# New rates for TensorE in the clock that weaves two stages of a four-layer network

## The chip, the cores and the metric

The kernel runs on one core of one Trainium2 chip. The metric is the device time of one execution in microseconds; several executions are timed and their median is taken. The core's engines are TensorE (PE, matrix products into PSUM), VectorE (DVE), ScalarE (ACT), GpSimd (POOL) and the sync engine (SP), from which most DMA transfers are issued. [...]

## The reference

The input `x` has shape (16, 32, 128, 128), float32. Four layers each add a function of the group-normalised `x` to `x`:

```python
x = x + _L0_conv_ref(_gn(x), ...)   # row LSTM over skewed columns, 128 steps
x = x + _L1_conv_ref(_gn(x), ...)   # adder convolution 3x3 on quantised values
x = x + _L2_conv_ref(_gn(x), ...)   # 2-D Hartley transform, 32x32 modes mixed, back
x = x + _L3_conv_ref(_gn(x), ...)   # edge operators, conv1..conv7, pools, deconvs
```

The adder convolution computes, for each image, output channel f and pixel,

```python
out[n, f, i, j] = -sum over c, kh, kw of |q[n, c, i + kh, j + kw] - qw[f, c, kh, kw]|
```

with `q` and `qw` rounded to whole numbers between -127 and 127. The last layer normalises five edge operators of `x`, applies a 3x3 convolution to their 160 channels, three levels of max pooling with 3x3 convolutions, three 2x2 deconvolutions with 3x3 convolutions behind them, and multiplies the result by its input.

## The kernel before, in words

**Stages.** `stage0` computes the LSTM layer; it is over before the part that matters here. `rest` computes the other three layers. The adder convolution is done by `Differences`, the Hartley layer and the last layer by `After`.

**The maps.** An image is handled in two halves of 64 rows. For each half there are 72 maps (8 blocks of output channels by 9 taps), 16 x 2 x 72 = 2304 in all. A map is `max(q - w, 0)` of a tile of 128 partitions by 8192 or 8320 float16 values, made either by DVE (line 760, tile `d_dve`, three buffers) or by ACT (line 757, tile `d_act`, two buffers). For each map PE adds it up over channels with sixteen matmuls into four PSUM banks (`sums`, line 647). Nine times per half `linear` adds the part that is linear in `q` (line 662, sixteen matmuls). `keep_busy` puts matmuls with zero weights (line 677) where PE would stand idle: four to a bank, at most four banks a map. After the 72nd map `finish` adds the residual, collects statistics and stores the rows of `x2`.

**The two last layers.** `After.work` is a Python generator. Images are taken in four groups of four. For a group it goes through `forward` (transform: lines 1119, 1134, 1091), `mixing` (line 1206), `back` (lines 1270 and 1315), `statistics` (line 1420: products of rows, from which the variances of the edge operators come), the table of folded weights `wf` (lines 1551, 1553), `conv1` (a 5x5 convolution of 25 taps, line 1739, in 8 chunks of 16 rows, with edge parts at lines 1713 and 1756), the smaller convolutions (`conv`, line 1589), and the composed deconvolutions with their convolutions (`Composed.round`, lines 905 and 930), the last of which, in `last`, gives the output (lines 1868 and 1838). A group can begin only when its four images have come out of the adder convolution: `yield ("after", 4 * g + 3)`.

**What sets the order.** The order of the instructions on every engine is fixed when the program is written out. `Differences.run` keeps a clock for each engine: `weave.dve` and `weave.act` grow by `DVE_US` = 2.36 and `ACT_US` = 7.15 for each map, and a map goes to the engine that would end it first. `weave.pe` grows by `PE_US` for the sums of each map. After each map `weave.advance(due)` lets the generator of `After` go on as long as a further step fits on PE before the next sums are due:

```python
start = max(self.pe, self.ready)
if start + 1.0 > due + SLACK:
    return
us = self.step()
```

A step is what lies between two `yield`s. A positive number yielded is the time in us that the step's matmuls take on PE; it is added to `weave.pe`. A negative number is a wait of that many us before the generator goes on. `SUMMED` is a wait for PE's results. Work of DVE, ACT and SP that belongs to a step (evictions, loads, stores) is written out with the step or put off by `weave.later(us, step)`. `keep_order` then ties each engine to the order written. All numbers are the planner's[...].

Groups 0 to 2 are given to this weave; group 3 cannot be in it, since its images are the last. `drain(weave, end.weave)` writes out what is left of the weave and group 3, step by step, whichever of the two is behind on its own clock. When one of them is through, the other is `alone`: it then uses the PSUM banks of both and splits its evictions between DVE and ACT.

Of the kernel before, what the change touches and what calls it, by code (L numbers as in the profile page):

```python
# [483 lines left out]

DVE_US, ACT_US, PE_US = 2.36, 7.15, 1.0
LATE = 1.5
SLACK, CLOCK = 3.0, 1.0
SUMMED = ("summed",)  # L490
# [29 lines left out]
class Differences:  # L520
# [134 lines left out]
    def linear(self, acc, q, tap):  # L655

        kh, kw = tap // 3, tap % 3
        for j in range(4):
            for k in range(4):
                rows = slice(32 * k, 32 * k + 32)  # L660
                row = 16 * j + 4 * k + kh
                self.nc.tensor.matmul(
                    acc[k][32 * j : 32 * j + 32, :],
                    self.sel16[rows, 8, :],
                    q[rows, row : row + 4, kw : kw + W],
                    start=False,
                    stop=False,
                )
        self.weave.pe = max(self.weave.pe, self.weave.now) + 0.45

    def keep_busy(self, acc, q, until):


        start = max(self.weave.pe, self.weave.now)
        for k in range(min(int((until - start - 0.1) / 0.25), 4)):
            for j in range(4):
                self.nc.tensor.matmul(  # L677
                    acc[k][32 * j : 32 * j + 32, :], self.zero, q[:, :4, :W], start=False, stop=False
                )
            self.weave.pe = start + 0.25 * (k + 1)  # L680

    def run(self, tc, ctx, weave):
        nc, R, P = self.nc, self.R, self.P
# [149 lines left out]
class Composed:  # L833
# [60 lines left out]
    def round(self, src, n, acc, pick):  # L894

        nc, t = self.nc, self.t
        for tap in range(4):
            for j in range(4):  # L900
                par, row, rows, o = pick(j)
                top, left = row + par // 2 + tap // 2, par % 2 + tap % 2
                for blk in range(4):
                    part = slice(32 * blk, 32 * blk + 32)
                    nc.tensor.matmul(  # L905
                        acc[blk][32 * j : 32 * j + 32, o : o + rows * n],
                        t[part, 4 * par + tap, :],
                        src[part, top : top + rows, left : left + n],
                        start=tap == 0,
                        stop=tap == 3,  # L910
                        skip_group_check=True,
                    )
            yield rows * n / 512 * 0.2 + 0.95
            if tap != 2:
                continue
            for j in range(4):
                par, row, rows, o = pick(j)
                pr, pc = par // 2, par % 2
                col = o + pc * (n - 1)
                parts = [(2 + pc, slice(col, (rows - 1) * n + col + 1, n), rows)]  # L920
                if row == 0 and pr == 0:
                    parts += [(0, slice(o, o + n), n), (4 + pc, slice(col, col + 1), 1)]
                if row + rows == n and pr == 1:
                    at = (rows - 1) * n
                    parts += [(1, slice(o + at, o + at + n), n), (6 + pc, slice(at + col, at + col + 1), 1)]
                for k, to, width in parts:
                    for blk in range(4):
                        part = slice(32 * blk, 32 * blk + 32)
                        b = self.bd[part]
                        nc.tensor.matmul(  # L930
                            acc[blk][32 * j : 32 * j + 32, to],
                            t[part, 16 + k, :],
                            bass.AP(b.tensor, b.offset, [list(b.ap[0]), [0, width]]),
                            start=False,
                            stop=False,
                            skip_group_check=True,
                        )
            yield 0.4
# [20 lines left out]
class After:  # L959
# [71 lines left out]
    def forward(self, g):  # L1031
# [4 lines left out]
        with self.pool("t_m") as mp:  # L1036
# [9 lines left out]
            with self.pool("t_t") as tp, ExitStack() as rows:  # L1046
# [39 lines left out]
                def second(n):  # L1086

                    p = self.acc()
                    for q in range(4):
                        lhs = t1s[n][:, 4 * q : 4 * q + 4, :].rearrange("p c k -> p (c k)")  # L1090
                        nc.tensor.matmul(p[:, 32 * q : 32 * q + 32], lhs, cst["cas"], start=True, stop=True)

                    def out():
                        xm = tp.tile([128, 4, M1], F32, name="xm", bufs=self.buffers["xm"])
                        nc.vector.tensor_copy(xm.rearrange("p q k -> p (q k)"), p[:, :128])
                        weave.dve += 0.3
                        first = xm_d.offset + (4 * g + n // 2) * 32768 + 16384 * (n % 2)
                        to = bass.AP(xm_d.tensor, first, [[32, 128], [4096, 4], [1, 32]])

                        def store():  # L1100
                            nc.sync.dma_start(to, xm)
                            steps[n] = None
                            if n % 2:
                                steps[n] = weave.later(4.0, lambda: self.modes(g, n // 2, tp, xs, steps))

                        steps[n] = weave.later(2.0, store)

                    steps[n] = outs[n] = weave.summed(out)
                    return 1.45

                yield -4.0
                t1s, ta, ready = {}, {}, {}
# [2 lines left out]
                def first(n):  # L1115
# [8 lines left out]
                        weave.dve += 0.7  # L1124

                    ready[n, 0] = weave.summed(out)
                    return 1.05

                def turned(n):

                    weave.done(ready[n, 0])
                    p = self.acc()
                    for a in range(4):
                        nc.tensor.transpose(p[:, 128 * a : 128 * a + 128], ta[n][:, a, :], cst["ident128"])
                    ready[n, 1] = weave.summed(lambda: scaled(n, p))
                    return 1.5

                for n in range(10):
                    if n < 8:
# [56 lines left out]
    def mixing(self, g, xs, wp, wt):  # L1196
# [5 lines left out]
        for ky in range(M1):  # L1202
# [9 lines left out]
                )  # L1212
            if ky % 4 == 3 and len(wt) < M1 // 4:
                wt.append(self.weights(wp, len(wt)))
            yield 1.0
            if ky % 4 == 3 and 8 < ky < M1 - 1 and not weave.draining:
                yield -2.5
        yield SUMMED
        zs = wp.tile([128, 2, 4, 4, 32], F32, name="zs", bufs=1)
        for half in range(2):  # L1220
# [12 lines left out]
    def back(self, g, load):  # L1233
# [6 lines left out]
        with self.pool("t_z") as zp_, self.pool("t_r", ahead) as rp:  # L1240
# [23 lines left out]
            for oh in range(2):  # L1264
                pa = [self.acc() for _ in range(4)]
                for o in range(16):
                    for r in range(4):
                        for blk in range(4):
# [5 lines left out]
                                start=True,  # L1274
                                stop=True,
                            )
                    yield 1.1
                yield SUMMED
                for blk in range(4):
                    dst = o1[:, :, blk, 16 * oh : 16 * oh + 16].rearrange("p h o -> p o h")  # L1280
# [28 lines left out]
            for n in range(16):  # L1309
                s, half = n // 2, n % 2  # L1310
                pf = [self.acc() for _ in range(2)]
                for i in range(4):
                    for r in range(2):
# [5 lines left out]
                            start=True,  # L1319
                            stop=True,  # L1320
                        )
                yield 0.8
                if previous:
                    yield -3.2
                    take_out(*previous)
# [67 lines left out]
    def statistics(self, g, pool, frames, sides, out, tables):  # L1393
# [35 lines left out]
        for ch in range(H // 16):  # L1429
# [3 lines left out]
            for l in range(2, 18):  # L1433
# [7 lines left out]
                first, last = len(own), min(H - r, 3)  # L1441
                if first < last:
                    products(xp, l, slice(l + first, l + last), 64, 68 * first, False, r == H - 3)
                yield 0.5
                if l not in (9, 17):
                    continue

# [117 lines left out]
    def small_layers(self, cp, rp, y1, y2):  # L1565
# [11 lines left out]
        def conv(src, n, name, evict):  # L1577
            rows = min(n // 4, 512 // n)
            for r in range(0, n, 4 * rows):
# [3 lines left out]
                for tap in range(9):  # L1583
                    kh, kw = tap // 3, tap % 3
                    for j in range(4):
                        for blk in range(4):
# [6 lines left out]
                                start=tap == 0,  # L1593
                                stop=tap == 8,
                            )
                    yield rows * n / 512 * 1.0 + 0.15
                yield SUMMED
                for blk in range(4):
                    evict(r, rows, acc[blk][:, : rows * n], blk)
# [83 lines left out]
    def conv1(self, g, pool, frames, y1, sides, wf, b1):  # L1683
# [19 lines left out]
        for s, n in enumerate("lr"):  # L1703
            for tap in range(11):
                for j in range(4):
                    for blk in range(4):
# [11 lines left out]
                            stop=tap == 10,  # L1718
                            skip_group_check=True,
                        )  # L1720
                yield 0.6
        yield SUMMED
        cut = pool.tile([128, 4, 2, 8, 4], F32, name="cut")
        for blk in range(4):
# [4 lines left out]
        for ch in range(H // R):  # L1729
# [4 lines left out]
            for tap in range(25):  # L1734
# [11 lines left out]
                if edge and tap == 23:  # L1746
                    n, j, first, row = edge
                    for part, col, wide in ((n, 0, 5), (n + "l", 1, 2), (n + "r", W + 1, 2)):
                        width = W if wide == 5 else 1
                        o = first + (W - 1 if part == n + "r" else 0)  # L1750
                        for cut_tap in range(2 * wide + 1):
                            for blk in range(4):
# [8 lines left out]
                                    stop=False,  # L1761
                                    skip_group_check=True,
                                )
                            yield 0.3
                yield 1.15
            yield SUMMED
            if ch + ahead < H // R:
                for half in range(2):
# [275 lines left out]
```

## Time and profile before

| What | Value |
|---|---|
| Median of 3 runs | 6719.5 us (6713.72 to 6728.77) |
| Profiled execution | 6728.15 us |
| Its span, first to last instruction | 6726.4 us |
| Mean granted clock of TensorE | 0.919 |
| PE, DVE, ACT busy | 5379.0, 5537.9, 5464.8 us (80%, 82%, 81%) |
| Maps on DVE, on ACT | 1675 of 2360 ns, 629 of 7154 ns |
| `keep_busy` matmuls | 6720 |

The span can be cut by the sums of the maps (line 647), which run from 685 us to 5603 us: before them lies `stage0`, after them the drain. The groups' first transform matmuls (line 1119) start at 1838, 3434, 5029 and 5666 us. In the profile's counts an instruction on float32 operands appears as two matmuls, so that a tap of conv1, sixteen matmuls in the code, is x32. Busy times of PE are of pipelined matmuls with modelled ends: the distance from start to start tells what one costs. "PEld" is PE's loading of weights; "issue" is time in which an engine waited for nothing that the profile shows.

### The profile page before, as it was taken

The page shows a single profiled execution, that of the slowest core. Times are in us where ns is not written, and L with a number is a line of the kernel's source. Part 1 is how long each engine was busy: PE and PEld are TensorE (multiplying, and loading weights), DVE is VectorE, ACT ScalarE, POOL GpSimd, SP SyncE. Part 2 cuts the span into 40 slices and gives each one's busy share as a digit, 9 for nine tenths or more (in the row PEclk, how much of TensorE's full clock was granted, in tenths as well). Part 3 has the DMA queues.
Part 4 walks back from the last instruction along what each step waited for, and adds up shares of the span by engine and source line. Part 5 has one row for each costly group of instructions (what it writes and reads, how often), then busy time and mean ns, then how long its engine had stood idle before and what let it go on. Part 6 is the DMA issues. An engine that isn't in the chain of part 4 may idle for free.

```text
span 6726.4 us, 271378 instructions
## 1 busy us (share of the span) xinstructions
PE 5379.0 (80%) x127212; PEld 2798.3 (42%) x127212; DVE 5537.9 (82%) x6839; ACT 5464.8 (81%) x3210; POOL 63.0 (1%) x67
## 2 busy tenths in 40 slices
PE   3798777788777879997877878998787785886896
PEld 3675333333343433333333433333334442453574
DVE  7898999999999889998999989999899995144122
ACT  3998999999999989999999999999899993121112
POOL 0000000000000000000000000000000000000000
PEclk9999899999989989998999889999899897997897
DMA  7553312212253632213453552221354353355314
GB/s 318 204 190 123 81 49 64 61 31 66 71 140 113 178 94 60 62 38 72 101 147 93 174 149 68 66 63 42 87 128 138 103 155 119 125 188 141 83 39 107
DMA packets 380776, 728.20 MB, mean 108 GB/s; under 512 B 73284, under 2 KB 225348, under 8 KB 368772
## 3 DMA queue, kind: packets, MB, share of 16 engines
q1 hardware_dynamic: 372180, 676.41, 35.2%
q0 software_dynamic: 7040, 33.80, 1.5%
q8 instruction: 995, 16.30, 1.0%
q14 instruction: 129, 1.06, 0.1%
q10 hardware_dynamic: 432, 0.64, 0.0%
HBM read 510.69 MB, written 200.00 MB: 106 GB/s over the span
## 4 chain that ended last, share of the span: by engine, by line
issue 33%; PE 29%; DVE 20%; ACT 14%; DMA 3%; SPq 1%; POOL 0%; DVEq 0%; ACTq 0%; POOLq 0%
DVE d_dve L760 12%; PE acc L1739 11%; ACT d_act L757 9%; PE acc L647 8%; PE acc L905 3%; PE pg L223 3%; ACT gt L237 2%; DMA v<-fold_d 1%; PE acc L1589 1%; PE acc L1420 1%; ACT junk L198 1%; DVE y L1677 1%; DVE stat L124 1%; DMA x_in<-in_x_dram 1%; ACT th L247 1%
## 5 line engine op out<-in xcount | busy, mean ns | idle before, releaser
L757 ACT ACTIVATE d_act<-q,neg 128x8192 f16<-128x8192 f16 (+1 forms) x629 | 4450.5, 7154 | 102.7 <-PE acc L647 81.1
L760 DVE TENSOR_SCALAR d_dve<-q,qw 128x8192 f16<-128x8192 f16 (+1 forms) x1675 | 3864.3, 2360 | 214.5 <-PE acc L647 195.6
L647 PE MATMUL acc<-d_dve,sel 128*32 128x512 f16 x26800 | 1879.4, 404 | 436.3 <-DVE d_dve L760 344.6
L647 PEld LDWEIGHTS <-sel 128*32 128x32 f16 x36864 | 1021.0, 101 | 2124.4 <-issue 1475.8
L1739 PE MATMUL acc<-xp,wf 32*32 32x512 f32 x25600 | 1001.7, 611 | 32.6 <-issue 27.2
L647 PE MATMUL acc<-d_act,sel 128*32 128x512 f16 x10064 | 740.0, 416 | 345.2 <-ACT d_act L757 333.4
L1680 ACT ACTIVATE y<-pooled,b 32x128 f32<-32x128 f32 x472 | 188.7, 400 | 552.6 <-DVE pooled L1666 546.3
L1739 PEld LDWEIGHTS acc<-xp,wf 32*32 32x32 f32 x25600 | 417.6, 104 | 377.6 <-issue 295.8
L677 PE MATMUL acc<-q,zero 128*32 128x512 f16 x6720 | 484.2, 400 | 0.0
L905 PE MATMUL acc<-y,u_conv 32*32 32x256 f32 (+1 forms) x9728 | 358.7, 461 | 85.1 <-issue 68.7
L223 PE MATMUL pg<-h,wb 64*64 64x20 f32 (+15 forms) x8192 | 342.0, 306 | 58.0 <-DVE h L251 32.9
L237 ACT ACTIVATE gt<-pg,bias 128x20 f32<-128x20 f32 (+15 forms) x1024 | 332.7, 385 | 39.3 <-PE pg L223 37.1
L223 PEld LDWEIGHTS pg<-h,wb 64*64 64x64 f32 x8192 | 252.1, 151 | 133.5 <-DVE h L251 80.9
L677 PEld LDWEIGHTS <-zero 128*32 128x32 f16 x6720 | 200.6, 101 | 187.3 <-issue 42.7
L1868 DVE SCALAR_TENSOR_TENSOR xr<-acc,l_one,xr 128x512 f32<-128x512 f32 x128 | 87.2, 744 | 229.8 <-PE acc L905 179.7
L1420 PE MATMUL acc<-xp 32*64 32x204 f32 (+3 forms) x8576 | 240.8, 339 | 40.6 <-issue 40.5
L905 PEld LDWEIGHTS acc<-y,u_conv 32*32 32x32 f32 x9728 | 162.0, 109 | 216.9 <-issue 168.1
L1420 PEld LDWEIGHTS acc<-xp 32*64 32x64 f32 (+1 forms) x8576 | 169.1, 132 | 124.4 <-issue 118.9
L1838 ACT ACTIVATE xr<-xr,l_ms 128x1024 f32<-128x1024 f32 x64 | 68.7, 1146 | 182.1 <-DVE xr L1868 171.9
L223 PE MATMUL pg<-xn,wb 64*64 64x2 f32 (+63 forms) x4096 | 183.5, 290 | 25.6 <-issue 17.0
L1774 DVE TENSOR_TENSOR acc<-acc,cut 128x4 f32<-128x4 f32 x256 | 35.2, 164 | 200.6 <-PE acc L1739 198.3
L1589 PE MATMUL acc<-y,w_conv 32*32 32x512 f32 (+2 forms) x4608 | 153.6, 487 | 37.1 <-issue 28.9
(218 smaller groups left out, 3624.5 us busy)
## 6 DMA issues: line engine op xcount, KB each, us to landing
q<-q_d SPq DMA_DIRECT2D x128, 536.2 KB, 10.3
xp<-xn_d SPq DMA_DIRECT2D x64, 660.0 KB, 5.1
xp<-x_d SPq DMA_DIRECT2D x56, 640.0 KB, 5.3
xr<-xn_d SPq DMA_DIRECT2D x64, 528.0 KB, 11.3
x_in<-in_x_dram SPq DMA_DIRECT2D x16, 2048.0 KB, 14.7
xn<-in_xs_dram SPq DMA_DIRECT2D x64, 512.0 KB, 7.1
res<-in_x_dram SPq DMA_DIRECT2D x64, 512.0 KB, 8.6
x_d<-res SPq DMA_DIRECT2D x64, 512.0 KB, 4.8
```

The source lines that it names most:

```text
L223: nc.tensor.matmul(bank[c][q][64 * pair : 64 * pair + 64, :, :width], wb[half, 4 * kind + KIND[q]].rearrange("p b o -> p (b o)"), v[half], ...
L237: nc.scalar.activation(gt[:, q, :, :n], bank[c][q][:, :, :n], AF.Tanh if q == G else AF.Sigmoid, bias=bias[:, KIND[q] : KIND[q] + 1],)
L647: self.nc.tensor.matmul(acc[k][32 * j : 32 * j + 32, :], self.sel16[:, i // 9, :], d[:, row : row + 4, c : c + W], start=first, stop=last,)
L677: self.nc.tensor.matmul(acc[k][32 * j : 32 * j + 32, :], self.zero, q[:, :4, :W], start=False, stop=False)
L757: nc.scalar.activation(dst, src, AF.Relu, bias=self.neg[:, i : i + 1])
L760: nc.vector.tensor_scalar(dst, src, self.qw[:, i : i + 1], 0.0, ALU.subtract, ALU.max)
L905: nc.tensor.matmul(acc[blk][32 * j : 32 * j + 32, o : o + rows * n], t[part, 4 * par + tap, :], src[part, top : top + rows, left : left + ...
L1420: nc.tensor.matmul(gram[blk][j : j + width, at : at + n], xp[part, l, 2 + j : 2 + j + width], xp[part, rows, j : j + width + 4], start=sta ...
L1589: nc.tensor.matmul(acc[blk][32 * j : 32 * j + 32, : rows * n], wc[name][part, tap, :], src[part, at : at + rows, kw : kw + n], start=tap == 0,
L1680: nc.scalar.activation(d, s, AF.Identity, bias=bj)
L1739: nc.tensor.matmul(acc[blk][32 * j : 32 * j + 32, :], tap_of("all", tap)[rows], xp[rows, 4 * j + kh : 4 * j + kh + 4, kw : kw + W], start= ...
L1868: nc.vector.scalar_tensor_tensor(v, acc[blk].rearrange("p (b r w) -> p r w b", b=2, w=64), one[:, blk : blk + 1], v, ALU.add, ALU.mult,)
```

## The change

Only the numbers by which the planner's clock counts PE change; no operation is added to the computation or taken from it. `PE_US`, the price of the sums of a map, goes from 1.0 to 0.88; `linear` from 0.45 to 0.36; a bank of `keep_busy` from 0.25 to 0.22, as a price and as the measure of how many fit. The positive numbers that the steps of `After` yield are replaced: 1.45 to 1.2, 1.05 to 0.9 and 1.5 to 1.0 in `forward`; 1.0 to 0.3 in `mixing`, where the wait after every fourth step goes from 2.5 to 5.5; 1.1 to 0.35 and 0.8 to 0.4 in `back`; 0.5 to 0.38 in `statistics`; in `conv1` 1.15 to 1.06 for a tap, 0.6 to 0.35 and 0.3 to 0.1 for edge parts; and the two formulas of the smaller convolutions and deconvolutions both become `rows * n / 512 * 0.78 + 0.28`.

```diff
-DVE_US, ACT_US, PE_US = 2.36, 7.15, 1.0
+DVE_US, ACT_US, PE_US = 2.36, 7.15, 0.88
...
-        self.weave.pe = max(self.weave.pe, self.weave.now) + 0.45
+        self.weave.pe = max(self.weave.pe, self.weave.now) + 0.36
...
-        for k in range(min(int((until - start - 0.1) / 0.25), 4)):
+        for k in range(min(int((until - start - 0.1) / 0.22), 4)):
...
-            self.weave.pe = start + 0.25 * (k + 1)
+            self.weave.pe = start + 0.22 * (k + 1)
...
-            yield rows * n / 512 * 0.2 + 0.95
+            yield rows * n / 512 * 0.78 + 0.28
...
-                    return 1.45
+                    return 1.2
...
-                    return 1.05
+                    return 0.9
...
-                    return 1.5
+                    return 1.0
...
-            yield 1.0
+            yield 0.3
             if ky % 4 == 3 and 8 < ky < M1 - 1 and not weave.draining:
-                yield -2.5
+                yield -5.5
...
-                    yield 1.1
+                    yield 0.35
...
-                yield 0.8
+                yield 0.4
...
-                yield 0.5
+                yield 0.38
...
-                    yield rows * n / 512 * 1.0 + 0.15
+                    yield rows * n / 512 * 0.78 + 0.28
...
-                yield 0.6
+                yield 0.35
...
-                            yield 0.3
-                yield 1.15
+                            yield 0.1
+                yield 1.06
```

## The prediction

> **What bounds the kernel now.** I read the slices of the span first: they show three regimes.
>
> ```profile
> PE   3798777788777879997877878998787785886896
> DVE  7898999999999889998999989999899995144122
> ACT  3998999999999989999999999999899993121112
> PEclk9999899999989989998999889999899897997897
> ```
>
> From slice 5 to slice 33 VectorE and ScalarE are both full; in the last seven neither is. By first and last start of line 647 the woven stage runs from 685 to 5603 us (4918 us), and what follows, which I call the drain, from 5603 to 6726 (1123 us). The busy times by stretch say what each is limited by (columns: length, busy us of PE, PEld, DVE, ACT, POOL, then granted clock, DMA share, GB/s):
>
> ```profile
> 685.00:1813.00 1128.00, 880.27 (x15604) 423.40 (x15607) 1111.90 (x844) 1104.16 (x171) 0.00 (x0) 0.94 0.22 55
> 2476.00:3027.00 551.00, 529.60 (x11706) 201.74 (x11704) 514.80 (x330) 534.37 (x189) 0.00 (x0) 0.97 0.20 52
> 685.00:5603.00 4918.00, 4042.93 (x86607) 1869.43 (x86610) 4642.39 (x3878) 4760.38 (x1165) 48.93 (x38) 0.92 0.35 92
> 5603.00:6727.00 1124.00, 870.06 (x28302) 552.41 (x28294) 333.47 (x911) 190.46 (x372) 11.67 (x22) 0.87 0.41 117
> 6437.00:6543.00 106.00, 105.46 (x3365) 90.22 (x3366) 21.32 (x76) 12.80 (x32) 0.00 (x0) 1.00 0.05 16
> ```
>
> The weave is bound by the 2304 maps that DVE and ACT share, 94% and 97% busy. The second row is the 5x5 convolution (conv1) of the first group of images: there PE is at 96% too. The fourth row, the drain, has no full engine: it is a chain. The costliest groups give the maps' prices, and the waits of the weave show how far PE already holds up DVE:
>
> ```profile
> L757 ACT ACTIVATE d_act<-q,neg 128x8192 f16<-128x8192 f16 (+1 forms) x629 | 4450.5, 7154 | 102.7 <-PE acc L647 81.1
> L760 DVE TENSOR_SCALAR d_dve<-q,qw 128x8192 f16<-128x8192 f16 (+1 forms) x1675 | 3864.3, 2360 | 214.5 <-PE acc L647 195.6
> ```
>
> In the timeline inside conv1 each map's sixteen sums (647) alternate with one tap (1739), without a gap:
>
> ```profile
> 2644.60 1.14 PE L1739 MATMUL acc<-xp,wf 32*32 32x512 f32 x32
> 2645.67 1.06 PE L647 MATMUL acc<-d_dve,sel 128*32 128x512 f16 x16
> 2646.66 1.15 PE L1739 MATMUL acc<-xp,wf 32*32 32x512 f32 x32
> 2647.74 1.05 PE L647 MATMUL acc<-d_dve,sel 128*32 128x512 f16 x16
> ```
>
> Start to start, tap plus map is 2.05 us; two maps in a row cost 0.87 us for the second.
>
> [...] I read PE's need from start-to-start spacing, not from its 96%. [...] The trace agrees: its records hold 1.0 and 0.5 only, mostly in pieces of 3.4 us. [...] in the drain the last group's line 1069 ran at 5659, 14 us after its input of 5645, behind line 1713.
>
> **The change part by part.** It alters no arithmetic, only the clock by which the Weave places background steps. (a) Sums 1.0 to 0.88 and linear 0.45 to 0.36 leave more planned PE time per map. (b) Background steps become cheaper (conv1 tap 1.15 to 1.06, deconvolution round 1.05 to 0.67 at 256 columns, mixing 1.0 to 0.3 with its pause 2.5 to 5.5, and so on). (c) keep_busy counts 0.22 instead of 0.25. So background steps stand closer together. The order of the two programs, counted in maps issued so far on PE, shows how far this goes:
> - Before, the groups begin at maps 587, 1305 and 2025 of 2304; each needs some 718, and the third has only ended its statistics when the maps are out. Its conv1 and all behind it fall into the drain.
> - After, they begin at 587, 1162 and 1739, end at 1105, 1678 and 2257: some 520 maps each. All three fit. The drain holds only the last group.
> - Totals are equal but for 3168 more keep_busy matmuls, one map shifted from ACT to DVE, and 24 evictions shifted likewise.
>
> Weave, worked out. In the map-only stretch 587 maps take 1128 us, 1.92 us each; 2304 maps are 4424. Group 0 from 1809 to 3399 is 1590 us for 718 maps: 1590 - 1379 = 211 us beyond its maps; group 1 likewise (1596 for 720 maps) 214; the part of group 2 in the weave then 4918 - 4424 - 425 = 69. Three whole groups instead cost 212 - 69 = **143 us more**. The rows confirm the size: the lines from wf to the output have 125 us of DVE and 81 us of ACT per group; traded at 2.36 and 7.15 us a map that is 0.75 x 125 + 0.25 x 81 = 114, the rest is idle time.
>
> Then the saturation of PE. Conv1 lies beside 209 maps where it had 267. By DVE and ACT alone its stretch would be 551 - 62 x 1.92 = 432 us (271 maps in the window shown). PE needs 200 pairs at 2.05 = 410, 9 more maps at 0.87 = 8, edge taps 14 (7 us for each of two), 26 linear steps at 0.37 = 10: 442, over the granted 0.97 = 456. PE is now the bound: 24 us, and some 6 us because PE will still stand now and then for a late map (in the 551 us it is idle 21 now). I take 30 x 3 = **90 us**; ends 0 and 180. In the other stretches PE's need stays under DVE's: statistics 49 x 0.97 + 128 x 0.45 = 105 us, over 0.91 = 115, against 173 - 27 x 1.92 = 121.
>
> The 198 extra keep_busy blocks of 16 are 0.87 us each, 172 us of PE. 71 of them lie in the first 587 maps: 62 us into a stretch where PE is 880 of 1128 busy. The idle PE hides them, cost 0; 40 us if they come late there. Weave: 143 + 90 = 233 us longer.
>
> Drain, phase by phase for the last group, by the first starts of its lines, with the other group's work gone from PE, DVE and the DMA queues:
> - 5603 to mixing at 5757, 154 us. The statistics chain takes 25 us in the weave (1813 to 1838) where it took 56 here; 8 images with loads and modes ran 91, I estimate 60. 7 + 25 + 60 = 92: **62 saved**.
> - Mixing to back's first matmul at 5841, 84 us. 32 steps at 0.45 are 14, then copies 3 and two small transfers and their gaps, about 18: 35. **49 saved**.
> - Back to the normalising at 6019, 178 us. Two halves of 1270 with evictions about 25; 16 residual steps, where DVE needs 2.7 us each and 1 MB must move (178 GB/s in that stretch now), 4 us each, 64; statistics and loads 26: 115. **63 saved**.
> - Statistics and weights to conv1 at 6247, 228 us. Line 1420 128 x 0.45 = 58, with loads 85 instead of 144; 1484 19; inverse root, folded tables and line 1713 56 of 64: 160. **68 saved**.
> - Conv1 to 6543, 296 us. Alone it already ran 25.3 us a chunk (6438, 6466, 6491, 6517): 8 x 25.4 + 8 = 212. **84 saved**.
> - From 6543 to 6726 group 3 is alone already: nothing.
>
> Sum 326, a drain of 798. Ends: 220 if loads, not the other group, paced the middle phases; 380. It is an estimate from rows of a mixed stretch, the least sure term.
>
> Sum: 6726 + 233 - 326 = 6633 against the profiled span of 6726.4 (its execution 6728.15). The median shown, 6719.5, is 0.13% lower; the same difference gives **6626 us**.
>
> **The rivals.**
> - *Larger gain.* The pairs are absorbed, conv1 does not saturate: 143 - 326, **6537 us**. For: in the 551 us of conv1 DVE waits only 29.9 us, 20 times, for PE's sums now. Against: the gapless pairs.
> - *The drain is the last group's own chain.* Then PE and DMA of the other group were in its gaps, and 230 us are saved at most: 233 - 230, **6723 us**. For: no engine is full there, DMA waits of ACT (63 us) remain, and a lone chain meets the half clock more (0.50 in 5604 to 5668). Against: conv1's 84 us are seen directly, and 5.5 us per residual step at line 1315 are five taps of the other group.
> - *Slower: TensorE overcommitted.* The place is conv1's stretch, three times. If each loses over 61 us instead of 30 (an effective pair of 2.2 us instead of 2.05), the drain's saving is spent; at 90 us each, 143 + 270 - 326 = +87, **6806 us**. For: plan and price differ, 0.88 + 1.06 = 1.94 against 2.05, and d_dve has three buffers, d_act two. Against: conv1 now holds its 551 us with the same pairs.
> - *No effect* is excluded: the programs differ by a whole group's work before the last map.
>
> **How the numbers follow.** Likeliest case 0.65, its own range 6560 to 6690; larger gain 0.17; own chain 0.10; overcommitted 0.08. The range 6520 to 6720 leaves out most of the last two and the tail of the second. Runs shown spread 0.2%, so about 0.2% can be told: below 6706 lies nearly all of the first two, 0.81; within 0.05, mostly the own-chain case; slower 0.14, the rest of it and the overcommitted one.
>
> **What would show it.** Right: the last map near 5603 + 233 = 5836, no conv1 of the third group behind it; drain near 800; the wait of d_dve for PE's sums above 195.6, most of it in three conv1 stretches of about 460 us with PE full. Wrong: a weave under 5760 (saturation priced too high) or over 5930, or a drain over 900, with waits on loads or half clock where I put the other group's matmuls.

## The result, and the profile after

The changed kernel takes 6786.0 us in the median (6783.25 to 6804.39), the kernel before 6718.8: a ratio of 1.0104 (of the means of four runs each), interval 1.0083 to 1.0125. It is 1% slower; 6626 us and a gain were forecast. In the profiled execution the last sum of a map ends at 6035 us instead of 5604, and the drain takes 750 us instead of 1122. So the move took place and the drain shrank by more than forecast (372 us instead of 326), but the weave grew by 429 us instead of 233.

The slices of the span show it: DVE and ACT, both full before, now have gaps in many slices of the weave.

```profile
PE   3697788888877799988777899788877999865696
DVE  7897999999988788888998888889877888873222
ACT  3898999999999889989988889889877899850012
PEclk9998899999999899989989999899988999985797
```

The busy times by stretch (columns as before: length, then PE, PEld, DVE, ACT, POOL, clock, DMA share, GB/s). The second row is conv1 of the first group, the last two are the weave and the drain:

```profile
685.00:1806.00 1121.00, 922.76 (x16689) 448.46 (x16692) 1107.34 (x838) 1101.01 (x170) 0.00 (x0) 0.96 0.22 55
2351.00:2823.00 472.00, 460.41 (x10536) 182.43 (x10540) 408.27 (x278) 422.19 (x169) 0.00 (x0) 0.98 0.20 54
685.00:6037.00 5352.00, 4519.03 (x101616) 2141.11 (x101615) 4778.94 (x4176) 4848.71 (x1324) 45.57 (x45) 0.93 0.34 91
6037.00:6785.00 748.00, 500.38 (x16456) 398.03 (x16456) 225.11 (x639) 101.65 (x188) 7.94 (x15) 0.78 0.44 130
```

The map-only stretch is what it was. DVE falls from 94% to 89% of the weave and ACT from 97% to 91%. The groups of the maps say for whom they wait:

```profile
L757 ACT ACTIVATE d_act<-q,neg 128x8192 f16<-128x8192 f16 (+1 forms) x628 | 4454.9, 7149 | 344.8 <-PE acc L647 320.2
L760 DVE TENSOR_SCALAR d_dve<-q,qw 128x8192 f16<-128x8192 f16 (+1 forms) x1676 | 3877.5, 2360 | 452.3 <-PE acc L647 431.5
```

DVE waits 431.5 us for sums (195.6 before), ACT 320.2 (81.1). The sums are late: PE has not yet read the buffers that the next maps need.

Where? I cut the weave at the first map after each stage's beginning on PE, and took off 1.92 us per map; conv1 runs here from its first tap to its last. What is left, in us, is what the stage costs beyond its maps:

| Stage | before, groups 0, 1 | after, groups 0, 1, 2 |
|---|---|---|
| forward | 20, 20 | 20, 21, 23 |
| mixing | -1, 1 | 15, 13, 21 |
| back | 37, 35 | 49, 44, 46 |
| statistics | 24, 26 | 34, 39, 47 |
| weights and edges (to the first tap) | 29, 29 | 32, 39, 39 |
| conv1 | 28, 24 | 64, 59, 63 |
| small convolutions to conv4 | 30, 29 | 28, 31, 25 |
| deconvolutions and output | 43, 47 | 66, 74, 55 |
| maps alone until the next group | 3, 3 | -5, -5, -10 |
| sum | 213, 214 | 303, 315, 308 |

Before, a further 69 us of group 2 lay in the weave: 496 in all, now 926. Conv1 lost about what was forecast. The surprise is in stages for which no loss was forecast: mixing, back, edges, statistics and the deconvolutions.

One of these, group 2's `back` in the timeline of PE, shows what happens:

```profile
4809.00 1.28 PE L1270 MATMUL acc<-cw,zi 32*32 32x32 f32 x128 [0.29 <-issue]
4819.07 1.53 PE L1270 MATMUL acc<-cw,zi 32*32 32x32 f32 x128 [8.79 <-issue]
4822.55 0.33 PE L1270 MATMUL acc<-cw,zi 32*32 32x32 f32 x6 [1.95 <-issue]
4822.81 1.90 PE L647 MATMUL acc<-d_act,sel 128*32 128x512 f16 x16
4824.50 1.59 PE L647 MATMUL acc<-d_dve,sel 128*32 128x512 f16 x16
```

PE runs 128 small matmuls in 1.3 us and then stands for 8.8 us, waiting for nothing that the profile can name. The sums behind them stand in the same queue and start at 4822.81. The waits of the same stretch give the bill:

```profile
DVE d_dve L760 <- PE acc L647: 12.3, 1, 12.3
PEld acc L1270 <- issue: 12.3, 5, 8.9
PE acc L1270 <- issue: 11.0, 3, 8.8
ACT d_act L757 <- PE acc L647: 8.3, 1, 8.3
```

In the drain, where nothing else is on PE, such stops show undisturbed in mixing:

```profile
6118.71 1.90 PE L1206 MATMUL acc<-xs,mix 128*32 128x8 f32 x128 [2.41 <-issue]
6122.47 1.94 PE L1206 MATMUL acc<-xs,mix 128*32 128x8 f32 x128 [1.86 <-issue]
6126.21 1.90 PE L1206 MATMUL acc<-xs,mix 128*32 128x8 f32 x128 [1.81 <-issue]
6129.96 1.90 PE L1206 MATMUL acc<-xs,mix 128*32 128x8 f32 x128 [1.85 <-issue]
```

After every 128 matmuls, each with its own weight load, PE stops; here each row of 128 begins 3.7 us after the one before (4.3 at the most in this stretch). The granted clock is 0.50. The shortest distance, 3.47 us, is found at this clock (in the drain's `back` from 6162.55 to 6166.02 us) and at the full one too, as in group 0's `back`, where the clock is 1.00 from 1998 to 2006 us:

```profile
2001.85 1.27 PE L1270 MATMUL acc<-cw,zi 32*32 32x32 f32 x128 [0.75 <-issue]
2005.32 1.34 PE L1270 MATMUL acc<-cw,zi 32*32 32x32 f32 x128 [2.20 <-issue]
```

Only the share of running and standing in it differs: 1.89 and 1.58 us at 0.50, 1.27 and 2.20 at 1.00.

What PE waits for can be read from the DMA records. One queue, q8, is called "instruction". All its packets have 16384 bytes, and in each of the fourteen profiles of this document their number is that of PE's matmuls and weight loads together, divided by 256, within 2: 995 packets for 254424 before, 1020 for 260760 here, 1003 for 256360 in the fastest version. By this count they are PE's instructions, 256 to a packet. In the mixing above, packets land at 6117.12, 6121.00, 6124.77 and 6128.58 us, and PE's rows of 128 begin 1.4 to 1.6 us after each. In the whole weave PE stands 87 times for 1 us or more with "issue" as the reason; 79 of these stops end 1.2 to 1.8 us after such a landing. Those 79 add up to 222 us, where the kernel before has 109.

The records also tell the long stops from the short ones. The lines below show how full the DMA engines were, in 40 slices of a window, and the packets of q8 in it. The first two are of the long stop in `back` (4809 to 4819.1 us), the last two of the mixing (6114.4 to 6137.7):

```profile
DMA  9993299390689929939099690699930225000000
q8 instruction: 1, 0.02, 0.8%
DMA  9997889931000001000000100000010000010000
q8 instruction: 6, 0.10, 1.8%
```

In the mixing, once a load at the start is over, the packets are the lone 1s and come in even steps. In `back` other transfers keep the DMA engines nearly full; the next packet starts only at 4816.23 us, as they end, and PE goes on at 4819.07. Of the 79 stops, 28 are longer than 2.6 us (129 us in all), and in 23 of them the DMA engines were over 90% busy from the stop's beginning until the packet started; of the 51 shorter ones (93 us) this holds for none. No run took those transfers away, so that they delay the packets is read from the traces and not shown by an experiment.

### The profile page after: what moved, and what is told of

It reads as the page before. It is cut to its first block, busy times and chain, and to the rows that moved or that the text cites. A ratio compares the mean times of both kernels' runs of the same rounds, so it can differ in the third digit from the quotient of the medians.

```text
span 6785.4 us, 277713 instructions
## 1 busy us (share of the span) xinstructions
PE 5483.6 (81%) x130380; PEld 2914.5 (43%) x130380; DVE 5565.9 (82%) x6864; ACT 5464.2 (81%) x3185; POOL 55.9 (1%) x67
## 3 DMA queue, kind: packets, MB, share of 16 engines
q8 instruction: 1020, 16.71, 1.0%
q14 instruction: 128, 1.05, 0.0%
## 4 chain that ended last, share of the span: by engine, by line
PE 40%; issue 27%; DVE 21%; ACT 7%; DMA 4%; SPq 1%; POOL 0%; DVEq 0%; ACTq 0%; POOLq 0%
PE acc L647 14%; PE acc L1739 13%; DVE d_dve L760 11%; ACT d_act L757 3%; PE acc L905 3%; PE pg L223 3%; PE acc L1589 2%; ACT gt L237 2%; DVE y L1677 1%; PE acc L677 1%; ACT junk L198 1%; DVE stat L124 1%; PE acc L1420 1%; PE acc L1270 1%; DMA v<-fold_d 1%
## 5 line engine op out<-in xcount | busy, mean ns | idle before, releaser
L757 ACT ACTIVATE d_act<-q,neg 128x8192 f16<-128x8192 f16 (+1 forms) x628 | 4454.9, 7149 | 344.8 <-PE acc L647 320.2
L760 DVE TENSOR_SCALAR d_dve<-q,qw 128x8192 f16<-128x8192 f16 (+1 forms) x1676 | 3877.5, 2360 | 452.3 <-PE acc L647 431.5
L647 PEld LDWEIGHTS <-sel 128*32 128x32 f16 x36864 | 996.3, 99 | 1980.2 <-issue 1289.7
L1739 PE MATMUL acc<-xp,wf 32*32 32x512 f32 x25600 | 955.1, 605 | 19.6 <-issue 17.9
L647 PE MATMUL acc<-d_act,sel 128*32 128x512 f16 x10048 | 718.6, 406 | 146.9 <-ACT d_act L757 122.6
L677 PE MATMUL acc<-q,zero 128*32 128x512 f16 x9888 | 682.1, 390 | 1.0 <-issue 1.0
L677 PEld LDWEIGHTS <-zero 128*32 128x32 f16 x9888 | 295.7, 99 | 261.7 <-issue 36.0
L905 PE MATMUL acc<-y,u_conv 32*32 32x256 f32 (+1 forms) x9728 | 308.0, 447 | 85.2 <-issue 73.2
L1365 ACT ACTIVATE xp<-xp,shift,stats 128x1280 f32<-128x1280 f32 (+1 forms) x64 | 91.6, 1434 | 311.2 <-DVE shift L1333 187.4
L223 PEld LDWEIGHTS pg<-h,wb 64*64 64x64 f32 x8192 | 251.1, 150 | 136.4 <-DVE h L251 81.1
L1420 PEld LDWEIGHTS acc<-xp 32*64 32x64 f32 (+1 forms) x8576 | 187.6, 142 | 136.9 <-issue 100.4
```

Of the source, the lines that this page charges most:

```text
L223: nc.tensor.matmul(bank[c][q][64 * pair : 64 * pair + 64, :, :width], wb[half, 4 * kind + KIND[q]].rearrange("p b o -> p (b o)"), v[half], ...
L647: self.nc.tensor.matmul(acc[k][32 * j : 32 * j + 32, :], self.sel16[:, i // 9, :], d[:, row : row + 4, c : c + W], start=first, stop=last,)
L677: self.nc.tensor.matmul(acc[k][32 * j : 32 * j + 32, :], self.zero, q[:, :4, :W], start=False, stop=False)
L757: nc.scalar.activation(dst, src, AF.Relu, bias=self.neg[:, i : i + 1])
L760: nc.vector.tensor_scalar(dst, src, self.qw[:, i : i + 1], 0.0, ALU.subtract, ALU.max)
L905: nc.tensor.matmul(acc[blk][32 * j : 32 * j + 32, o : o + rows * n], t[part, 4 * par + tap, :], src[part, top : top + rows, left : left + ...
```

## The experiments

Theories before the first runs. A: sums and steps are priced below what they cost side by side, so sums come late. B: the 3168 additional keep_busy matmuls hold up the sums. C: the late half of group 2 costs in the weave what the drain saves, however it is placed. The timelines above led to D after the first four runs: PE's instructions arrive in packets of 256, so a run of small matmuls is bound by 3.5 to 3.8 us a packet and not by its matmuls. (The packets' own records, told above, are the stronger evidence for this; the rows of 128 alone led to it.)

In what follows "weave" and "drain" are those of each run's profile; ratios are to the kernel before, run beside it on the same chip.

**The maps' rates alone.** All background steps keep their old prices.

```diff
-DVE_US, ACT_US, PE_US = 2.36, 7.15, 1.0
+DVE_US, ACT_US, PE_US = 2.36, 7.15, 0.88
...
-        self.weave.pe = max(self.weave.pe, self.weave.now) + 0.45
+        self.weave.pe = max(self.weave.pe, self.weave.now) + 0.36
...
-        for k in range(min(int((until - start - 0.1) / 0.25), 4)):
+        for k in range(min(int((until - start - 0.1) / 0.22), 4)):
...
-            self.weave.pe = start + 0.25 * (k + 1)
+            self.weave.pe = start + 0.22 * (k + 1)
```

> The new rates of the maps alone (sums 0.88, linear 0.36, keep_busy 0.22), the old prices of all background steps. The groups then begin at maps 586, 1237 and 1892, between the kernel before and the changed one. Theory A (background steps stand too close to the sums because the sums and steps are priced below what an alternating pair costs, so sums come late and DVE and ACT wait for their buffers): the density is in between, so is the time: 6720 to 6760 us, waits of d_dve for sums 250 to 350 us. Theory B (the extra keep_busy matmuls delay the sums): 8212 of them, half of the surplus of 3168, so about half of the excess over a weave without it, likewise 6730 to 6760. Theory C (bringing the third group's late half into the weave costs what the drain saves, however it is spaced): 6725 to 6745.

6663.8 us, ratio 0.9901 (0.9884 to 0.9917): faster than the kernel before, which no theory had. Weave 5019, drain 961; d_dve waits 231.9 us. This half of the change is a gain by itself. C falls: part of group 2's late half is in the weave at a profit.

**The steps' prices alone.** The changed kernel with sums at 1.0, linear at 0.45 and keep_busy at 0.25.

```diff
-DVE_US, ACT_US, PE_US = 2.36, 7.15, 0.88
+DVE_US, ACT_US, PE_US = 2.36, 7.15, 1.0
...
-        self.weave.pe = max(self.weave.pe, self.weave.now) + 0.36
+        self.weave.pe = max(self.weave.pe, self.weave.now) + 0.45
...
-        for k in range(min(int((until - start - 0.1) / 0.22), 4)):
+        for k in range(min(int((until - start - 0.1) / 0.25), 4)):
...
-            self.weave.pe = start + 0.22 * (k + 1)
+            self.weave.pe = start + 0.25 * (k + 1)
```

> The other half of the change: new prices of the background steps, old rates of the maps (sums 1.0, linear 0.45, keep_busy 0.25). The groups begin at maps 586, 1171 and 1758 and the third just fits before the last map; 7108 keep_busy matmuls. Theory A: more room about each map's sums, so d_dve waits under 300 us for PE against 431.5 in the changed kernel, a weave near 5170 us instead of 5352, and 6600 to 6660 us in all. If the prices of the steps are the fault and not those of the sums: as the changed kernel, 6760 to 6800. Theory B: also better than the changed kernel, 6600 to 6680. Theory C: 6760 to 6800.

6707.7 us, ratio 0.9973 (0.9963 to 0.9982). Weave 5201, drain 813, d_dve waits 349.5. The time is in none of the ranges. Each half by itself is faster than the kernel before, both together slower: the two densities add up on PE. The waits stayed well above the 300 us of theory A, in spite of the dearer sums.

**keep_busy's price undone.**

```diff
-        for k in range(min(int((until - start - 0.1) / 0.22), 4)):
+        for k in range(min(int((until - start - 0.1) / 0.25), 4)):
...
-            self.weave.pe = start + 0.22 * (k + 1)
+            self.weave.pe = start + 0.25 * (k + 1)
```

> The changed kernel with one number undone: keep_busy counts 0.25 again. The groups' places stay as in the changed kernel to the map; 9264 keep_busy matmuls instead of 9888. Theory A: no difference, 6770 to 6800 us. Theory B: a fifth of the surplus of 3168 is gone, so 20 to 60 us less, 6725 to 6765. Theory C: no difference.

6774.2 us, ratio 1.0070 (1.0055 to 1.0085), in A's range and above B's. Against the changed kernel's 1.0104 (1.0083 to 1.0125) the intervals overlap.

**The sums' price undone.**

```diff
-DVE_US, ACT_US, PE_US = 2.36, 7.15, 0.88
+DVE_US, ACT_US, PE_US = 2.36, 7.15, 1.0
```

> The changed kernel with one number undone: the sums of a map are priced 1.0 again, the rest as changed. Groups begin at 586, 1178 and 1760, the third ends before the last map; 7496 keep_busy matmuls. Theory A: the sums' price is the one that counts most since it stands beside every step: as in the run with the old rates of all maps, 6600 to 6660 us, d_dve waits under 300 us. Theory B: 6600 to 6680 too. Theory C: 6760 to 6800.

6741.8 us, ratio 1.0020 (1.0010 to 1.0030). Weave 5240, drain 811, d_dve waits 346.5. Again no range holds it. A fair part of the loss is gone, but not the whole gain that A wanted. I added up the time that DVE and ACT waited for sums, by the background line that PE had begun last. At conv1's taps it falls from 259 us in the changed kernel to 170; at lines 1206, 1270 and 1713, whose steps are made of small matmuls, it does not fall (184 and 203). So room about the sums helps conv1 and not those lines.

**Old prices for the steps of small matmuls.** The changed kernel with

```diff
-            yield 0.3
+            yield 1.0
             if ky % 4 == 3 and 8 < ky < M1 - 1 and not weave.draining:
-                yield -5.5
+                yield -2.5
...
-                    yield 0.35
+                    yield 1.1
...
-                yield 0.4
+                yield 0.8
...
-                yield 0.35
+                yield 0.6
...
-                            yield 0.1
+                            yield 0.3
```

> The changed kernel with the old prices of the steps made of small matmuls: mixing 1.0 with its pause 2.5, back 1.1 and 0.8, conv1's edges 0.6 and 0.3. Sums, taps, deconvolution rounds, convolutions, statistics and keep_busy as changed. The third group then just ends with the last map. Theory D (PE's instructions arrive in packets; in a run of small matmuls PE stops after every 128 matmuls with their 128 weight loads, 3.5 to 3.8 us a packet at the least, so that a step of 32 matmuls costs 0.9 us and not the 0.3 that its matmuls take): the waits of DVE and ACT at lines 1206, 1270 and 1713, together 182 us in the changed kernel, fall to about 60; the weave shortens from 5352 to about 5230, in all 6680 to 6720 us. Theory A (only the sums and taps are too cheap): 6760 to 6790.

6727.2 us, ratio 1.0009 (1.0002 to 1.0016): seven us above D's range, far from A's. The waits at lines 1206, 1270 and 1713 fall from 184 us to 38 (49 in the kernel before), while those at conv1's taps stay (259 and 251). The weave is 5200 us (5346 before this edit), the drain 833. Part of this is a move and no gain: against expectation the end of group 2 falls into the drain again, as it does in the two runs with the sums at 1.0. The waits of this run's weave:

```profile
DVE d_dve L760 <- PE acc L647: 339.9, 220, 10.2
...
ACT d_act L757 <- PE acc L647: 240.9, 120, 11.2
```

**No keep_busy at all.**

```diff
-        for k in range(min(int((until - start - 0.1) / 0.22), 4)):
+        for k in range(min(int((until - start - 0.1) / 0.22), 0)):
```

> The changed kernel without any keep_busy matmul (they add zeros, so nothing computed is left out); all else in place. Theory B: the excess goes and more with it, 6620 to 6680 us. Theory A or D: the dummies fill what is idle anyway; the granted clock drops in the map-only stretches, the time is 6750 to 6810.

6767.0 us, ratio 1.0064 (1.0049 to 1.0079). The weave is 5329, d_dve waits 424.7 us: little changes, though all 9888 matmuls are gone and the granted clock falls from 0.917 to 0.887. They cost some 0.4%, not the 100 us and more that B asked for: B falls as the cause of the loss.

**Maps' rates alone, keep_busy at 0.25.** Only two numbers differ from the kernel before:

```diff
-DVE_US, ACT_US, PE_US = 2.36, 7.15, 1.0
+DVE_US, ACT_US, PE_US = 2.36, 7.15, 0.88
...
-        self.weave.pe = max(self.weave.pe, self.weave.now) + 0.45
+        self.weave.pe = max(self.weave.pe, self.weave.now) + 0.36
```

> As the run with the new rates of the maps alone (6664 us), but keep_busy at 0.25: only sums 0.88 and linear 0.36 are new. 7688 instead of 8212 keep_busy matmuls. Theory B: 10 to 30 us less, 6635 to 6655. Theories A and D: 6655 to 6672, the same.

6640.3 us, ratio 0.9874 (0.9860 to 0.9889), the fastest of all. It lies in B's range and below that of A and D; the last run below returns to this. Its weave is 67 us longer than before, its drain 158 us shorter:

```profile
685.00:5674.00 4989.00, 4204.21 (x92398) 1952.29 (x92397) 4685.89 (x3964) 4786.52 (x1228) 49.44 (x45) 0.94 0.34 93
5674.00:6638.00 964.00, 741.14 (x23482) 497.87 (x23474) 307.13 (x850) 156.19 (x284) 7.95 (x15) 0.82 0.44 124
```

DVE and ACT stay at 94% and 96% in the weave, close to the 94% and 97% of the kernel before.

**Maps' rates and conv1's tap.** The first experiment with

```diff
-                yield 1.15
+                yield 1.06
```

> The new rates of the maps and of conv1's tap (1.06), the old prices of all other steps. Groups begin at 586, 1225 and 1870. Differs from the run with the maps alone (6664 us) by the tap only. Theory A: conv1 is packed beyond what PE can do, so its stretch hardly shortens and DVE and ACT wait more there, 6670 to 6700 us. Theory D: the tap's matmuls are long enough for the packets to keep up, so the denser conv1 is worth what it brings in: 6635 to 6665.

6662.4 us, ratio 0.9911 (0.9896 to 0.9926): the same as without the tap. More of group 2 moves in (drain 929 instead of 961), the weave grows by nearly as much (5042 instead of 5019). Beside the old prices of the other steps, conv1's tap is neither a loss nor a gain; beside their new prices it was not tried alone.

**Mixing twice in the drain.** The changed kernel with

```diff
-                nc.tensor.matmul(
+                for _ in range(2 if weave.alone else 1):
+                    nc.tensor.matmul(
...
```

> The changed kernel, but in the drain every matmul of mixing (line 1206) of the last group is issued twice to the same place, so nothing computed changes: 1024 more matmul records with their 1024 weight loads, 8 packets of 128. In the changed kernel this stretch runs from 6110 to 6138 us with a stop of about 1.85 us after every 128 matmuls. Theory D (instructions come in packets at 3.5 to 3.75 us each): the stretch becomes 28 to 30 us longer, with a stop after every 128 again, and the drain with it. If the stops came from anything else (data, the half clock, the semaphores of the weights), the 1024 matmuls cost what their own runs take, 8 x 1.9 = 15 us at the half clock or 12 at the full one.

The stretch runs from 6130.4 to 6186.8 us, 56.4 instead of 28.3: 28 us for eight packets, 3.5 each, as theory D said. The drain is 39 us longer (789); the other 11 us are not explained by the added matmuls, and the ratio is 1.0157 (1.0141 to 1.0172). PE's timeline there:

```profile
6164.57 1.94 PE L1207 MATMUL acc<-xs,mix 128*32 128x8 f32 x128 [1.80 <-issue]
6168.04 1.95 PE L1207 MATMUL acc<-xs,mix 128*32 128x8 f32 x128 [1.53 <-issue]
6171.52 1.94 PE L1207 MATMUL acc<-xs,mix 128*32 128x8 f32 x128 [1.53 <-issue]
6175.26 1.94 PE L1207 MATMUL acc<-xs,mix 128*32 128x8 f32 x128 [1.80 <-issue]
```

The added matmuls use the same data and wait for nothing new, and the stop comes after every 128 again. The count of instructions set the time here. The instruction queue counts along: here are its lines for the changed kernel, for this run with 2048 instructions more, and for the run without keep_busy, with 19776 less.

```profile
q8 instruction: 1020, 16.71, 1.0%
q8 instruction: 1028, 16.84, 1.1%
q8 instruction: 943, 15.45, 0.9%
```

That is 8 packets more and 77 fewer, as 2048 / 256 and 19776 / 256 give. No run changed the size of a packet.

**Statistics at its old price too.** The run with the small matmuls' prices back, and

```diff
-                yield 0.38
+                yield 0.5
```

> As the run with the small-matmul prices back (6727 us), with statistics at 0.5 as well; sums, taps, rounds, convolutions and keep_busy stay as changed. A statistics step of 16 records takes 0.53 us from its start to that of other work in the trace, not 0.38. If its price carries a share of the rest of the loss: waits of DVE at line 1420 fall from 78 to about 40 us and the time to 6690 to 6710 us. If not (the rest lies with the rounds of line 905): 6720 to 6735.

6690.9 us, ratio 0.9928 (0.9913 to 0.9943), as the first branch said. The waits of DVE at line 1420 fall from 78 to 42 us. Weave 5081, drain 917. PE's stops for packets, counted as above, add up to 110 us in this weave; they were 222 in the changed kernel, 161 in the run with the small matmuls' old prices, and 109 in the kernel before. What still separates this from the run with all prices but the tap's old (0.9911) are the rounds, the convolutions and forward; the intervals overlap.

**A little more of what does not stop.** The fastest version with rounds at `rows * n / 512 * 0.2 + 0.75`, convolutions at `rows * n / 512 * 0.9 + 0.2`, and forward's new prices.

```diff
-            yield rows * n / 512 * 0.2 + 0.95
+            yield rows * n / 512 * 0.2 + 0.75
...
-                    yield rows * n / 512 * 1.0 + 0.15
+                    yield rows * n / 512 * 0.9 + 0.2
...
-                    return 1.45
+                    return 1.2
...
-                    return 1.05
+                    return 0.9
...
-                    return 1.5
+                    return 1.0
```

> The fastest so far (sums 0.88, linear 0.36, else as before: 6640 us) with steps that have no long run of small matmuls priced lower: rounds of line 905 0.85 instead of 1.05, transform steps as changed, convolutions 1.1 instead of 1.15. Groups begin at 586, 1228 and 1857 instead of 586, 1233 and 1891, so some 30 maps' time of work moves out of the drain. If the room is there: 6615 to 6640 us. If PE is already as full as it can be: 6640 to 6665.

6675.5 us, ratio 0.9909 (0.9894 to 0.9924): slower than without, and above both ranges. The weave grew by 60 us for 19 us of drain; the waits of DVE at line 905 double, 27 to 56 us. Either the room is not there, or the pieces fell badly; the next run shows how much that can be.

**keep_busy at 0.28.** The fastest version with

```diff
-        for k in range(min(int((until - start - 0.1) / 0.25), 4)):
+        for k in range(min(int((until - start - 0.1) / 0.28), 4)):
...
-            self.weave.pe = start + 0.25 * (k + 1)
+            self.weave.pe = start + 0.28 * (k + 1)
```

> Sums 0.88 and linear 0.36, all steps as before, keep_busy at 0.28: the third point after 0.22 (6664 us) and 0.25 (6640 us). If keep_busy's price matters because a block that is planned too short holds up the next sums: 6620 to 6640. If 0.25 was enough, since 0.25 us is above the 0.216 that four zero matmuls take at the full clock: 6635 to 6655.

6668.9 us, ratio 0.9898 (0.9880 to 0.9916), outside both ranges. With 0.22, 0.25 and 0.28 at 0.9901, 0.9874 and 0.9898 there is no trend in the price, so the result in B's range at 0.25 does not speak for B. Group 1's conv1 takes 513, 481 and 511 us in the three, beside 238, 226 and 241 maps: where the pieces happen to fall seems to be worth some 20 us, and smaller differences between such plans should not be read as effects of a number.

## Why the prediction was wrong

**What bounds the kernel, and what moves: right.** The weave is bound by the maps; all three groups ended before the last map; the drain held group 3 alone. One reading beside this was too strong: the pieces of one clock in the trace of before, 170 at 1.0 and 170 at 0.5, are multiples of 3.413 us (339 of the 340, to 0.01 us), but only 127 are a single 3.413.

**The 143 us for the moved work.** No run separates it from the waits, so it stays an estimate. (The matmuls of line 647 begin at 687 us and not at 685; that changes the 1.92 us a map by 0.2%.)

**Conv1: right in size.** 462 us were worked out for 209 maps; from first to last tap the three stretches took 465, 455 and 457 beside 209, 206 and 205 maps. Up to the first convolution behind it PE was busy for 460 of 472 us. One slip in the working had no weight: the 432 us by DVE and ACT alone took 62 maps off a stretch that reached to that convolution (551 us, 271 maps); from tap to tap it is 540 us and 267 maps, hence 429. The sign to look for was wrong in part: the waits of d_dve were to lie mostly in conv1, but 160 of the 431.5 us do.

**"In the other stretches PE's need stays under DVE's": this step failed.** It was worked out only for statistics, with 6 us to spare, and for nothing else; statistics too came out at 34 to 47 us beyond its maps instead of 24 to 26. PE's need was counted in matmuls, as in the drain too ("32 steps at 0.45 are 14"), and the supply of its instructions was put at nothing. The trace of before already held the other price: conv1's edges at line 1713 took 31 us beside 9 maps in each of two groups, with "issue" pauses among the waits, and I passed over them. In a run of small matmuls alone 128 records took 3.47 us at the least, so I estimate a step of 32 at about 0.9 us. The old prices 1.0 and 1.1 of mixing and `back` carry just this; the new 0.3 and 0.35 are matmul time alone, so the planner packed three steps into the place of one, and the sums of the maps stood behind them. The stops with the DMA engines over 90% busy until the packet started lasted 2.7 to 8.8 us in the weave; no price held that either.

In the table mixing, back and edges cost 102 us more over three groups than at the rates of before, statistics 45, the deconvolutions 60, conv1 18 more than forecast, with 30 less in forward, the small convolutions and the gaps: together the 196 us by which the weave's 429 exceed the 233 of the sum. That small matmuls and statistics were priced too low is shown by the runs with their old prices, at the lines concerned. Not all of the 196 us is time in which PE stood for packets: those stops grew by 113 us (from 109 to 222). The rest seems to be PE with too much work planned beside the sums, as the relief of conv1 by dearer sums suggests; no run separates the shares.

**Keep_busy at nothing: nearly right.** Without any the weave is 17 us shorter.

**The drain: right in kind, short in size.** 798 us forecast, 750 measured. Mixing was priced too low (14, measured 28), and so were the two halves at line 1270 (25, measured 38); conv1 was nearly right (212, measured 217). The surplus lies elsewhere before conv1: 75 us up to mixing where 92 were forecast, and 238 from `back` to the first tap where 275 were. So the other group had probably held these up more than I took off; no run shows it.

**The rivals.** The overcommitted PE was the case that came, with 0.08; but its place was wrong. It named conv1 and a pair of 2.2 us; conv1 came out as worked out, and over half of the unforeseen loss (102 of 196 us) lay in steps of small matmuls, where PE stood without instructions while its busy time looked as if there were room. "Own chain" and "larger gain" did not come.

What stays open: whether the other transfers delay the packets. In the changed kernel the stops with full DMA engines last up to 8.8 us in the weave and up to 5.1 in the drain, but no run moved those transfers. Nor does any run isolate what the rounds of lines 905 and 930 lose: their price was changed together with others each time.

## What to carry to other kernels

A price for a planner must be the distance from the start of a step to the start of the next piece of work in a row of such steps, not the time that its instructions are busy: here 0.9 us, estimated from the 3.47 us a row, against 0.3. When the releaser of an idle time is "issue" and it comes after a fixed number of instructions, count instructions, not operand sizes, and set the landings of the instruction queue's packets beside the stops. And a plan that fills one engine to its real rate has little room for errors in the order: the fastest version here took half of the step, new rates for the sums and old prices for what lies between them.

## What the runs showed of the hardware

- By their count, PE's instructions came in packets of 16384 bytes, 256 instructions each: in all fourteen profiles the packets of q8 are PE's instructions divided by 256, within 2 (995 for 254424 before, 1020 for 260760 in the changed kernel). Of PE's 87 "issue" stops of 1 us or more in the changed kernel's weave, 79 ended 1.2 to 1.8 us after a packet had landed.
- In rows of 128 small matmuls with their 128 weight loads the shortest distance from row to row was 3.47 us, at a granted clock of 1.00 (2001.85 to 2005.32 in the changed kernel) and of 0.50 (6162.55 to 6166.02 there). Twice the matmuls on the same data took 28 us for eight more packets.
- Of the 79 stops, the 23 with the DMA engines over 90% busy until the packet started are all longer than 2.6 us, up to 8.8; none of the 51 shorter ones is of this kind.
- Taking away all 9888 zero matmuls lowered the granted clock from 0.917 to 0.887 and did not lengthen the kernel (6767.0 us against 6786.0).
